# A graph layer on Trainium2: 29 or 35 of the node windows summed by matmul, the rest by gathered rows

## The chip, the cores and the metric

The kernel runs on one core of one Trainium2 chip. The metric is the device time of one execution in microseconds (us). Three runs of the kernel before gave 547.09, 547.55 and 548.72 us, median 547.55 us. The profiled execution is the one of 548.72 us.

## What is computed

There are 6,250 nodes with 128 features each and 100,000 edges, sorted by destination. Each edge has a type, 0 or 1. Every edge sends a linear image of its source's row, with one of two weight matrices by its type. The messages are summed by destination, the node's own image is added, and a ReLU, a residual and a layer norm follow:

```python
m_data = Xs @ W_data.T + b_data          # Xs = X[src]
m_ctrl = Xs @ W_control.T + b_control
msg = jnp.where((edge_types == 0)[:, None], m_data, m_ctrl)
agg = jax.ops.segment_sum(msg, dst, num_segments=X.shape[0])
out = jax.nn.relu(agg + (X @ W_self.T + b_self))
x = layernorm(x + out)
```

All of it is float32 in the reference.

## The kernel before, in words

**Preparation.** The images of all 6,250 nodes under both weight matrices are made first (L424 to L478). Each value is kept as three bfloat16 parts, so a row has 384 numbers. The rows lie in 98 blocks of 128: 49 blocks of nodes by two types. They stay in the on-chip tensor `m3`, and a copy goes to the tensor `table` in HBM (L476).

**Two ways of summing.** The nodes are divided in two. The first `NW` windows of 160 nodes each are summed by matmuls alone; the nodes behind them are summed in blocks of 128 by gathered rows.

*A window* (function `ranks`, then `sums`). Its edges (2,688 loaded, 21 to a partition) are first given places. The sort of L588 to L826 is done for a *group* of up to four windows at once. It walks 21 steps: DVE makes a one-hot mask of the source block of each edge (L644), PE adds it up against a triangle of ones (L654, eight matmuls of up to 392 columns in each step but the last, which has four), and DVE takes each edge's rank among the edges of the same block (L658). Masks at L673 and L679 and the scatter at L688 turn ranks into a list of 32 places for each source block, which goes to HBM and comes back as a broadcast to all partitions (`rows`, L838, 784 KB a window). Edges beyond 32 places, at most 64 a window, are listed by L725 to L791 and their rows are fetched by GpSimd (L796). The sums of one window then run over 25 sets of four source blocks:

- DVE turns the broadcast into masks (L846, two instructions a window) and makes the masks of destinations (L853, five a window);
- first stage, L866: four matmuls of 384 columns, each on a quarter of PE's columns, pick the rows of the edges out of `m3`;
- ACT copies the result from PSUM to SBUF as bfloat16 (L407; the planner may give it to DVE instead, L408);
- second stage, L880 and L883: four matmuls of 384 columns and three of 128 add the rows up by destination in the PSUM tile `a`.

There are two tiles `a` and three tiles `g` for the first stage.

*A gathered block* (function `gathered`, L902). Its edges are loaded as tiles of 128; a full block has 18 tiles. For each tile GpSimd fetches 128 rows of `table` by index (L958), six in flight, and PE adds them up by destination with four matmuls of 384 columns (L965) into the single PSUM tile `ga`. DVE makes the masks for six tiles at a time (L952). Eight short DVE instructions (L919 to L935) prepare up to four full blocks at once.

*The end of a window or block* (function `close`): DVE adds the three parts (L528), adds the residual (L537), takes the statistics (L541, L543) and a chain of short instructions (L554 to L567) makes the scale; ACT or DVE apply it (L572 to L579), and SP stores the result. In a group of windows the short chain is shared by four or five pieces, and in a gathered block it stands alone. The last 32 nodes of each window are closed together, one extra piece for each group but the first.

**The order of the work** is set at build time. Every operation is given to `Plan` (L84 to L188) with an engine, an estimated duration and a due time, and `Plan.run` simulates the engines and issues the operations in the order it finds. Windows are due every `TW` = 13 us. The sort of a group is due 58 us ahead of its first window and takes 1.8 us a step there. The gathered tiles are spread evenly between the third window and the last but one:

```python
g0, g1 = T0 + 2 * TW, T0 + (NW - 2) * TW
step = max((g1 - g0) / max(sum(GT), 20), 1.3)
```

**The numbers that the change touches** (L35 to L47):

```python
GROUPS = [1, 2] + [4] * 6 + [2]
NW = sum(GROUPS)
NGB = -(-(N - NW * WN) // P)
GT = [-(-(min(P, N - NW * WN - P * i) * 17) // P) + 1 for i in range(NGB)]
```

So there are 9 groups, 29 windows with 4,640 nodes, and 13 gathered blocks with the other 1,610 nodes: twelve of 128 nodes and 18 tiles, and one of 74 nodes and 11 tiles, 227 tiles in all. At the very end the matched edges are counted; were an edge not placed, the slow function `sums_over_all` would run over everything (L220 to L222).

Of the kernel before, what the change touches and what calls it, by code (L numbers as in the profile page):

```python
# [31 lines left out]
WN = 160  # L32
KT = 21
WIN = KT * P
GROUPS = [1, 2] + [4] * 6 + [2]  # L35
NW = sum(GROUPS)
R = 32
W4 = WN - P
# [45 lines left out]
class Plan:  # L84
# [6 lines left out]
    def add(self, engine, dur, fn, due, r=(), w=(), lat=0.0):  # L91
        alts = engine if isinstance(engine, list) else [(engine, dur, fn)]
        op = Op(alts, due, lat)
        op.index = len(self.ops)
        self.ops.append(op)
        deps = set()
        for items, writes in ((r, False), (w, True)):
            for item in items:
                b, key = item if isinstance(item, tuple) else (item, None)
                for k, (ws, rs) in b.keys.items():  # L100
                    if key is None or k is None or k == key:
                        deps.update(ws)
                        if writes:
                            deps.update(rs)
                if writes and key is None:
                    b.keys = {}
                ws, rs = b.keys.setdefault(key, ([], []))
                if writes:
                    b.keys[key] = ([op], [])
                else:  # L110
                    rs.append(op)
                if not b.users or b.users[-1] is not op:
                    b.users.append(op)
        deps.discard(op)
        op.deps = list(deps)
        return op
# [115 lines left out]
def sums_over_windows(ctx, tc, x, xt, edges, w, bias, out, total):  # L232
# [10 lines left out]
    table = dram.tile([NT * P, D3], BF16, name="table")  # L243
    packed = dram.tile([len(GROUPS), 2, P, NT], BF16, name="packed")

# [3 lines left out]
    def C(shape, dtype, name):  # L249
        return Buf(plan, const, shape, dtype, name, 1)  # L250
# [22 lines left out]
    def vec(due, cols, fn, r, w, rate=1.04):  # L273
        return add("DVE", dve(cols, rate), fn, due, r, w)
# [54 lines left out]
    for i in range(3):  # L329
        vec(0.3, P, lambda i=i: V.memset(one3.t[R * i : R * i + 1, :], 1.0), [], [one3], 0.3)  # L330
    counts = C([P, len(GROUPS) + NGB], F32, "counts")
    vec(2, 1, lambda: V.memset(counts.t, 0.0), [], [counts])
# [569 lines left out]
    def gathered(bis, when, step):  # L902

        nt, k_ = GT[bis[0]], len(bis)
        n = nt * k_
        gi = len(GROUPS) + bis[0]
        top = GB * max(GT)
# [67 lines left out]
    todo = []  # L975
    for gi, nw in enumerate(GROUPS):
        if gi == 0:
# [26 lines left out]
    total_ps = low()  # L1004
    nt = len(GROUPS) + NGB
    add("PE", 0.1, lambda: T.matmul(total_ps.t[:1, :nt], ones.t, counts.t, start=True, stop=True),
# [145 lines left out]
```

## Time and profile before

| | before |
|---|---|
| median of three runs | 547.55 us |
| profiled execution, its own time | 548.72 us |
| its span in the trace | 546.8 us |
| mean granted TensorE clock | 0.962 |
| PE / PEld busy | 483.3 / 380.5 us |
| DVE busy | 463.3 us, 1,615 instructions |
| ACT busy | 387.0 us |
| POOL busy | 252.2 us |
| 227 gathers of `t_msg` on POOL | 1,036 ns each |

PE is the matmul engine, PEld its weight loads, DVE the vector engine, ACT the scalar engine, POOL GpSimd, SP the engine that issues the transfers. Busy time is the union of an engine's instructions, so two that overlap are counted once. A group of instructions is shown as line, engine, operation, output and inputs with their shapes and count, then busy time and the mean duration of one in ns, then the idle time of the engine just before them and what ended it. A view by stages gives the busy time of each engine in stretches of the span, with the count of its instructions behind an x. The page's own chain of work that ended last is empty for this run.

### The profile page before, as it was taken

To read this page: it belongs to the slowest core of one execution; us is meant where nothing else is said; L and a number is where in the kernel's file an instruction comes from. 1 tells how busy PE (TensorE), PEld (TensorE's weight loads), DVE (VectorE), ACT (ScalarE), POOL (GpSimd) and SP (SyncE) were. 2 spreads that over 40 slices of the span, in tenths; PEclk is the share of its full clock that TensorE was granted. 3 is DMA by queue.
4 is the path that set the end of the run, shared out by engine and by line. 5 is a ranking of instruction groups with operands and counts; after the bars stand their busy time and mean duration, and the time that the engine had idled before them with its cause. 6 is when DMAs were issued, how large, how long until landed. Compare 5 with 4: busy or idle time off the path is not lost.

```text
span 546.8 us, 28398 instructions
## 1 busy us (share of the span) xinstructions
PE 483.3 (88%) x11972; PEld 380.5 (70%) x11972; DVE 463.3 (85%) x1615; ACT 387.0 (71%) x981; POOL 252.2 (46%) x251
## 2 busy tenths in 40 slices
PE   4996597998899899997999989998999999999891
PEld 2664364675578778786777777886778778887771
DVE  6885688899999999999999999899989987778603
ACT  2684464675577867777786877777777878888891
POOL 2000026413115766666556666566657667576000
PEclk9998888798799999999999999999999989999997
DMA  2689756404532474526652265426544265436100
GB/s 84 176 236 286 215 175 193 144 4 115 184 115 65 112 241 111 155 69 201 176 167 78 70 210 177 145 74 194 167 119 126 73 203 164 133 82 203 38 7 18
DMA packets 62714, 75.25 MB, mean 138 GB/s; under 512 B 19726, under 2 KB 52659, under 8 KB 62579
## 3 DMA queue, kind: packets, MB, share of 16 engines
q1 hardware_dynamic: 50497, 49.00, 28.7%
q0 software_dynamic: 11648, 23.87, 16.6%
q8 instruction: 95, 1.56, 1.2%
q10 hardware_dynamic: 434, 0.49, 0.3%
q14 instruction: 40, 0.33, 0.2%
HBM read 58.71 MB, written 13.20 MB: 132 GB/s over the span
## 4 chain that ended last, share of the span: by engine, by line


## 5 line engine op out<-in xcount | busy, mean ns | idle before, releaser
L407 ACT CAST gs<-g 128x384 bf16<-128x384 f32 x684 | 293.2, 480 | 89.5 <-PE g L866 81.3
L958 POOL DMA_INDIRECT t_msg<-table,t_idx x227 | 235.1, 1036 | 163.5 <-PE ga L965 93.6
L866 PE MATMUL g<-m,rows 128*32 128x384 bf16 x2842 | 272.3, 332 | 1.7 <-DVE rows L846 1.4
L880 PE MATMUL a<-gs,hot 128*32 128x384 bf16 x2784 | 264.2, 331 | 9.4 <-ACT gs L407 5.5
L866 PEld LDWEIGHTS <-rows 128*32 128x32 bf16 x2842 | 177.2, 135 | 17.3 <-DVE rows L846 2.8
L883 PE MATMUL a<-gs,hot 128*32 128x128 bf16 x2088 | 167.2, 220 | 1.1 <-issue 1.1
L880 PEld LDWEIGHTS <-hot 128*32 128x32 bf16 x2900 | 124.0, 96 | 36.5 <-issue 17.0
L658 DVE TENSOR_REDUCE slot<-rk 128x4 f32<-128x392 f32 (+2 forms) x189 | 90.4, 478 | 24.3 <-PE rk L654 19.8
L965 PE MATMUL ga<-t_msg,t_hot 128*32 128x384 bf16 x897 | 91.5, 331 | 2.3 <-DVE s L528 2.3
L883 PEld LDWEIGHTS <-hot 128*32 128x32 bf16 x2175 | 83.9, 97 | 7.1 <-issue 2.7
L654 PE MATMUL rk<-hots,tri 128*32 128x392 bf16 (+2 forms) x756 | 73.8, 309 | 7.6 <-DVE hots L644 7.6
L853 DVE TENSOR_TENSOR hot<-iota_b,to_d 128x800 bf16<-128x800 bf16 x145 | 76.6, 565 | 0.0
L654 PE MATMUL rk<-hots,rest 128*32 128x392 bf16 (+2 forms) x720 | 66.1, 311 | 9.6 <-DVE slot L658 8.4
L796 POOL DMA_INDIRECT sr<-table,at x15 | 14.4, 957 | 81.8 <-DVE t_far L931 65.8
L654 PEld LDWEIGHTS <-rest 128*32 128x32 bf16 x720 | 30.2, 96 | 31.1 <-issue 26.8
L644 DVE TENSOR_TENSOR hots<-iota_b,st 128x392 bf16<-128x392 bf16 (+2 forms) x189 | 51.3, 314 | 0.4 <-PE vt L688 0.2
L965 PEld LDWEIGHTS <-t_hot 128*32 128x32 bf16 x897 | 41.9, 98 | 6.7 <-issue 3.6
L654 PEld LDWEIGHTS <-tri 128*32 128x32 bf16 x756 | 32.4, 98 | 11.0 <-DVE tri L313 6.9
L846 DVE TENSOR_SCALAR rows<-rows,pid 128x1568 bf16<-128x1568 bf16 x58 | 37.8, 672 | 0.4 <-DMA rows<-packed 0.4
L528 DVE TENSOR_REDUCE s<-a 128x128 f32<-128x384 f32 x29 | 16.0, 553 | 24.8 <-ACT bs L407 15.2
L688 PEld LDWEIGHTS <-two 128*64 128x64 bf16 x609 | 16.0, 110 | 11.7 <-DVE two L679 5.8
L444 PE MATMUL g<-w_sb,xc 128*128 128x256 f32 x60 | 21.8, 454 | 2.2 <-DMA xc<-in_xt 2.2
(179 smaller groups left out, 567.7 us busy)
## 6 DMA issues: line engine op xcount, KB each, us to landing
rows<-packed SPq DMA_DIRECT2D x29, 784.0 KB
table<-m SPq DMA_DIRECT2D x12, 768.0 KB
t_msg<-table,t_idx POOLq DMA_INDIRECT x227
xc<-in_xt SPq DMA_DIRECT2D x11, 256.0 KB
xc<-in_xt SPq DMA_DIRECT2D x6, 320.0 KB
xr<-in_x SPq DMA_DIRECT2D x6, 256.0 KB
out<-xr SPq DMA_DIRECT2D x6, 256.0 KB
gl<-sr SPq DMA_DIRECT2D x29, 48.0 KB
```

The costliest lines, as they stand in the source:

```text
L407: [("ACT", act(cols), lambda: A.copy(o(), src())), ("DVE", dve(cols), lambda: V.tensor_copy(o(), src()))], None, None, due, r, w, lat)
L444: T.matmul(o, xa.t[:, at : at + P], w_sb.t[:, : 2 * D], start=i == 0, stop=False, skip_group_check=True)
L644: vec(due - (2.0 if k else 0.5), nw * NT, lambda k=k, hot=hot, k0=k0: V.tensor_tensor(hot.t[:, k - k0].rearrange("p w (c d) -> p w c d", d=2),
L654: T.matmul(acc.t[R * j : R * j + R, : nw * NT], wt.t[:, R * j : R * j + R], m, start=start, stop=stop, skip_group_check=True)
L658: vec(due, nw * NT, lambda k=k: V.tensor_reduce(slot.t[:, k, :], acc.t[:, : nw * NT].rearrange("p (w c) -> p w c", c=NT), axis=AX.X, op=AL ...
L846: add("DVE", dve(half * NT, 0.26), lambda sp=sp, rs=rs: V.tensor_scalar(sp.t[:, rs], sp.t[:, rs], pid1.t, None, op0=ALU.is_equal), due - 4 ...
L853: V.tensor_tensor(hot2.t[:, c0 : c0 + 5].rearrange("p g (c d) -> p g c d", d=2), iota1_b.t.rearrange("p (c d) -> p c d", d=2)[:, None].to_ ...
L866: T.matmul(gp.t[R * t : R * t + R, :D3], sp.t[:, :, 4 * g + t], m3.t[:, 4 * g + t, :], start=True, stop=True)
L880: T.matmul(a.t[R * j : R * j + R, :D3], hot2.t[:, g, R * j : R * j + R], gs.t, start=g == 0, stop=False, skip_group_check=True)
L883: T.matmul(a.t[R * c : R * c + R, D3:], hot2.t[:, g, P:], gs.t[:, c * D : (c + 1) * D], start=False, stop=last, skip_group_check=True)
L958: add("POOL", 1.25, lambda m=m, kk=kk: G.indirect_dma_start(out=m.t, out_offset=None, in_=table[:, :], in_offset=bass.IndirectOffsetOnAxis ...
L965: T.matmul(ga.t[R * i : R * i + R, :D3], hot.t[:, k % KB, R * i : R * i + R], m.t, start=k == 0, stop=False, skip_group_check=True)
```

## The change

One line is changed. The group of two windows at the end becomes a group of four, and one more group of four is added.

```diff
-GROUPS = [1, 2] + [4] * 6 + [2]
+GROUPS = [1, 2] + [4] * 8
```

All else follows from it: 10 groups and 35 windows with 5,600 nodes; 6 gathered blocks with the other 650 nodes (five of 128 nodes and 18 tiles, one of 10 nodes and 3 tiles), 93 tiles in all. The gathered tiles are planned 4.3 us apart instead of 1.43 us: (33 - 2) x 13 us over 93 tiles, before (27 - 2) x 13 us over 227. The full blocks are prepared four at a time and then one, before in three batches of four. No other line of the kernel differs.

## Prediction

> **What bounds the kernel now.** I read the busy shares of the page first, then the span cut into stages, then the DVE groups and the waits of the long middle stage. The page:
>
> ```profile
> PE 483.3 (88%) x11972; PEld 380.5 (70%) x11972; DVE 463.3 (85%) x1615; ACT 387.0 (71%) x981; POOL 252.2 (46%) x251
> PEclk9998888798799999999999999999999989999997
> ```
>
> No engine is idle enough to be ignored except POOL. The stages say more. I cut where the first window's sum starts (70), where the fourth window's sum leaves PSUM (157), after 17 more windows (424), where the last sort and gather are over (510), and at the last window's end (534.8):
>
> ```profile
> core 0: us, PE busy (x) PEld busy (x) DVE busy (x) ACT busy (x) POOL busy (x), PEclk, DMA share, GB/s
> 70.00:157.00 87.00, 75.73 (x1807) 55.52 (x1809) 80.33 (x277) 54.16 (x144) 28.43 (x28) 0.87 0.42 127
> 157.00:424.00 267.00, 250.12 (x6814) 206.62 (x6806) 252.37 (x813) 201.03 (x516) 165.78 (x160) 1.00 0.48 140
> 424.00:510.00 86.00, 82.66 (x2310) 68.93 (x2309) 67.02 (x234) 71.94 (x189) 55.23 (x55) 0.98 0.47 138
> 510.00:534.80 24.80, 21.60 (x586) 16.85 (x577) 9.84 (x37) 21.23 (x56) 0.00 (x0) 1.00 0.07 18
> 534.80:546.80 12.00, 0.89 (x10) 0.54 (x10) 4.34 (x24) 1.25 (x5) 0.00 (x0) 0.69 0.08 20
> ```
>
> In the 267 us of the middle DVE is busy 252.4/267 = 94.5% and PE 93.7%, ACT 75%, POOL 62%. Only there are windows, sorts and gathers all under way. The DVE groups of that stage show what fills it:
>
> ```profile
> L658 DVE TENSOR_REDUCE slot<-rk 128x4 f32<-128x392 f32 x91 | 50.5, 555 | 1.3 <-PE rk L654 1.3
> L853 DVE TENSOR_TENSOR hot<-iota_b,to_d 128x800 bf16<-128x800 bf16 x85 | 44.7, 566 | 0.0
> L644 DVE TENSOR_TENSOR hots<-iota_b,st 128x392 bf16<-128x392 bf16 (+1 forms) x96 | 28.7, 341 | 0.1
> L846 DVE TENSOR_SCALAR rows<-rows,pid 128x1568 bf16<-128x1568 bf16 x34 | 22.8, 687 | 0.4 <-DMA rows<-packed 0.4
> L952 DVE TENSOR_TENSOR t_hot<-iota_b,t_code 128x768 bf16<-128x768 bf16 x25 | 13.8, 551 | 0.0
> L528 DVE TENSOR_REDUCE s<-a 128x128 f32<-128x384 f32 x17 | 9.4, 552 | 4.0 <-ACT bs L407 1.0 <-PE ga L965 0.9 <-PE rk L654 0.9
> L528 DVE TENSOR_REDUCE s<-ga 128x128 f32<-128x384 f32 x9 | 4.7, 525 | 0.0
> ```
>
> The L528 rows count the work: 17 windows and 9 gathered blocks closed, so a window takes 267/17 = 15.7 us there. Almost nothing of DVE's groups has idle time ahead of it. The waits of the same stage:
>
> ```profile
> POOL t_msg L958 <- PE ga L965: 64.1, 57, 21.8
> ACT gs L407 <- PE g L866: 42.6, 79, 1.4
> POOL t_msg L958 <- PE g L866: 32.6, 47, 2.4
> ```
>
> POOL waits for PE, not PE for gathered rows: gathering isn't the bound, and taking it away removes no wait from the path. **DVE sets the pace, with PE close behind.**
>
> **The prices on DVE.** An instruction starts before its predecessor has ended, so means over-count. Two L853 in a row took 1.05 us in the trace; the second added 0.49. I charge the long ones their mean less 0.08 us (L853 0.49, L658 0.475, L644 0.26, L846 0.61, L528 0.48, L952 0.47; the masks of L673 and L679, 0.50, at 0.44), L537 0.26, L541 0.27, L543 0.17, and the dependent short ones (L554 to L567, 0.13 to 0.17) whole.
> - A gathered block of 18 tiles: three L952 1.41, one close 0.45 + 0.26 + 0.27 + 0.17 = 1.15, the short chain 7 x 0.15 = 1.05, in all 3.6 us; a preparation of 8 short instructions, about 1.6 us, stands for up to four blocks.
> - A window's sum and close: 5 x 0.49 + 2 x 0.61 + 0.48 + 0.26 + 0.27 + 0.17 + 0.1 = 4.95 us.
> - The sort of a group of four: 21 x (0.475 + 0.26) = 15.4; four times three masks 5.3; some 35 others about 7.5; the group's shared close and its extra piece 1.9. In all 30 us.
> - A group of four in place of two: the 196-column forms of L658 and L644 stand at 354 and 252 ns on the page by form, the 392-column ones at 556 and 354, so 21 x 0.30 = 6.4, and 3 for the other masks and lists.
>
> **The sum over the kernel on DVE.** Added: 6 x 4.95 + 30 + 9.4 = 69 us, and about 2 for casts of L408 that the planner now puts on DVE (17 casts of L408 in the built program for 12). Removed: 22 instructions L952 (38 to 16), 10.3; seven closes and short chains, 7 x 2.2 = 15.4; one preparation, 1.6; in all 27. Net +44, so 463 to 507 us. ACT gets 150 more casts at 0.48, +72 gross, but it has the room. POOL loses 134 gathers and gains 2, -137: worth nothing by itself.
>
> **The sum on PE.** In the tail one set of a window (two times four matmuls of 384 columns, three of 128) passes every 0.38 us:
>
> ```profile
> 531.00 0.35 PE L880 MATMUL a<-gs,hot 128*32 128x384 bf16 x4
> 531.16 0.24 PE L883 MATMUL a<-gs,hot 128*32 128x128 bf16 x3
> 531.18 0.38 PE L866 MATMUL g<-m,rows 128*32 128x384 bf16 x4
> 531.38 0.35 PE L880 MATMUL a<-gs,hot 128*32 128x384 bf16 x4
> ```
>
> Four matmuls of 384 columns are 384/896 of that, 0.165 us, which is what a gathered tile costs. So six windows add 6 x 25 x 0.385 = 58 us and the removed tiles give back 134 x 0.165 = 22: a window needs 25 x 0.385/160 = 60 ns of PE per node, a full gathered block 18 x 0.165/128 = 23 ns. The change moves 960 nodes from the cheaper form to the dearer one on PE, DVE and ACT alike. Only POOL is relieved.
>
> **The end, by stages.** In the order of the built program PE has the same 18 gathered tiles and the same 71 sort steps up to the end of the fourth window, so **0 to 157 us stays**. The last sort is again over four or five windows before the end: 26 windows (the fifth to the thirtieth) with sorts beside them, then five without.
> - The 26 windows. Before, DVE had 252.4/17 = 14.85 us a window with 9 tiles. Without gathered work that is (252.4 - 25 x 0.47 - 9 x 2.2 - 4)/17 = 12.75; sorts are slightly thinner (5.13 steps a window by the built order, 5.26 before), -0.2; the 74 tiles left in this stretch, some 17 us over 26 windows, +0.65. So 13.2 us a window, 343 in all. PE, by the pace above, had 9.6 for the sets, 1.5 for 9 tiles, 5.26 x 2 x 392/896 x 0.385 = 1.8 for sort steps and, as I estimate from the counts, 1.4 for scatter, lists and own rows, 14.3 a window; it goes to 9.6 + 0.5 + 1.7 + 1.2 = 13.0. DVE was 94.5% busy with PE at 14.3/14.85 of it; now the two are closer, and I take 93.5%: 14.1 us a window, **367 us**.
> - Five windows without sorts. Before: 24.8 us for two, and 13 us for the one from 497 to 510, less 8 tiles at 0.165. About 12 us each, **60 us**. PE alone would need 25 x 0.385 + 0.7 = 10.3, the lower end.
> - The last close: **12 us**, the same chain.
>
> Sum 157 + 367 + 60 + 12 = 596 us of span; 1.9 us lie outside it (548.72 - 546.8), 598 against the profiled run's 548.7, which is 1.2 above the median. **Forecast: 597 us.** Cross-check: 507 us of DVE, less 49.4 before 70 (the same view) and some 30 after the sorts (9.8 for two windows now, 4.3 for the close), are 428 us in 157 - 70 + 367 = 454, 94%.
>
> Unseen before: groups that follow more densely on SP (6 more broadcasts of 784 KB, 4.7 MB, and 13 MB less gathered; DMA was 48% busy in the middle, so no cost), and gathered tiles that are few and come in bursts. What a window then waits for I bound by both ends: no slack lost (DVE 97% busy, 354 us) and no slack won (15.7 us a window as now, 408 us). I stay near the lower end, since almost no wait on PE or DVE names a gather.
>
> **A rule of the skill weighed.** L846 took 687 ns in the middle and 627 between 70 and 157, where POOL worked less; L853 566 and 564. By these rows, fewer gathers are worth 58 x 0.06 = 3.5 us at most. The Trainium skill, "SBUF — State Buffer", section "Who interferes with whom", says that some DVE instructions and GpSimd lock each other out of a shared port pair for a whole instruction; if each of the 134 gathers had held DVE up for its 1.04 us, 139 us would come back and the kernel would be faster. The rows show no such hold.
>
> **Rivals.**
> 1. *The gathers were free filler* (0.13): they filled holes that windows leave anyway, and a window stays at 15.7. 157 + 408 + 60 + 12 + 2 = 639; half of it, 618, is where it begins. For: PE and DVE both have 6% holes. Against: DVE's groups show no idle time that gathers could fill.
> 2. *PE and DVE pack better with fewer queues* (0.15): 13.3 us a window and 10.5 in the five last, 346 + 53 + 171 = 570.
> 3. *The other side* (0.02), one mechanism: DVE's instructions shrink in the middle for want of GpSimd's traffic. Not slower needs (547.5 - 157 - 60 - 12 - 2)/26 = 12.2 us a window, so DVE's 13.2 us shorter by 8% and no hole left. L853's 566 ns with gathers and 560 without (510 to 534) speak against it.
> 4. *It doesn't do what it says* (under 0.01): an added window might hold too many edges and the slow function run, milliseconds. The inputs settle it: of the added windows the fullest has 2,676 edges of 2,688, and at most 43 edges of 64 overflow the lists.
>
> **Chances.** The forecast 0.70, the others as given. The range takes in half of the filler case and the better packing: 570 to 617. A measurement of this kernel tells 0.3% from no change: faster 0.02, within 0.01, slower 0.97.
>
> **What would show it.** Right: some 14 us a window in the middle with DVE over 92% busy, DVE about 507 us in all, POOL about 116. Wrong: L853 or L658 shorter by several per cent (rival 3); a window at 15 us or more with DVE under 90% (rival 1); an early stage that no longer ends at 157.

## The result, and the profile after

The kernel after takes 614.43 us (median of four runs, 613.06 to 616.28), beside 548.13 us for the kernel before: a ratio of 1.1206, 95% interval 1.116 to 1.1252. The forecast was 597 us, in a range of 570 to 617. The profiled execution took 616.28 us, with a span of 614.6 us. The page of the kernel after, the rows that answer to those shown of before:

```profile
PE 536.3 (87%) x13418; PEld 422.3 (69%) x13418; DVE 506.8 (82%) x1681; ACT 446.9 (73%) x1134; POOL 118.2 (19%) x120
PEclk9999785999999999999999999999999999999996
```

All engines but POOL did more. DVE came to 506.8 us where the sum of instructions said 507, POOL to 118 where it said about 116. ACT gained 60 us where the sum said 72, and PE 53 where sets and tiles alone gave 58 - 22 = 36, a sum that left out the added sort steps. So the instructions of the engine that the forecast rests on were priced well, and the difference lies in how they fit together. The stages of the kernel after, cut at the same events (first sum, end of the fourth window, 424, end of the last window with a sort beside it, end of the last window); the columns are the stretch, its length, busy time and count of each engine, granted clock, DMA share and GB/s:

```profile
core 0: us, PE busy (x) PEld busy (x) DVE busy (x) ACT busy (x) POOL busy (x), PEclk, DMA share, GB/s
67.00:157.80 90.80, 78.76 (x1836) 56.96 (x1837) 79.75 (x278) 54.40 (x144) 27.73 (x28) 0.86 0.44 129
157.80:424.00 266.20, 247.64 (x6768) 204.02 (x6770) 248.62 (x785) 210.70 (x544) 63.45 (x61) 1.00 0.35 102
424.00:538.20 114.20, 105.42 (x2912) 88.54 (x2908) 97.19 (x293) 90.12 (x233) 23.34 (x22) 1.00 0.31 94
538.20:598.40 60.20, 54.95 (x1448) 41.99 (x1438) 27.69 (x83) 53.20 (x137) 0.95 (x1) 1.00 0.20 64
598.40:614.60 16.20, 0.88 (x16) 0.54 (x16) 4.03 (x18) 1.47 (x5) 0.00 (x0) 0.67 0.10 26
```

The start is as before (157.8 against 157.0). The 26 windows with sorts take 266.2 + 114.2 = 380.4 us, 14.63 each; DVE is busy 345.8 us of them, 90.9%. The five windows without sorts take 60.2 us, and the last close 16.2 us instead of 12.0. What DVE did in the 380 us, and whom it waited for:

```profile
L658 DVE TENSOR_REDUCE slot<-rk 128x4 f32<-128x392 f32 x137 | 76.4, 558 | 12.7 <-PE rk L654 9.8 <-PE ga L965 1.5 <-PE g L866 0.9
L853 DVE TENSOR_TENSOR hot<-iota_b,to_d 128x800 bf16<-128x800 bf16 x130 | 68.4, 562 | 0.0
L846 DVE TENSOR_SCALAR rows<-rows,pid 128x1568 bf16<-128x1568 bf16 x50 | 30.6, 642 | 3.8 <-DMA rows<-packed 3.8
L528 DVE TENSOR_REDUCE s<-a 128x128 f32<-128x384 f32 x25 | 13.8, 554 | 5.0 <-ACT bs L407 3.9 <-PE rk L654 0.6 <-PE a L883 0.3
```

The mean durations are those of before, to 1%, except L846 (642 ns for 687). The idle time ahead of L658 has grown. It is 12.7 us here, and in the answering stretch of before (157 to 497.2 us, 22 windows) 1.3 + 5.8 us, most of it in the last sort, a group of two windows:

```profile
L658 DVE TENSOR_REDUCE slot<-rk 128x4 f32<-128x392 f32 x95 | 52.7, 555 | 1.3 <-PE rk L654 1.3
L658 DVE TENSOR_REDUCE slot<-rk 128x2 f32<-128x196 f32 x21 | 7.4, 353 | 5.8 <-PE rk L654 5.5 <-issue 0.3
```

So in the sorts of four windows, where DVE hardly waited for PE before, it now does.

### The profile page after: what moved, and what is told of

It is laid out like the page before. It is cut to its first block, busy times and chain, and to the rows that moved or that the text cites. A ratio compares the mean times of both kernels' runs of the same rounds, so it can differ in the third digit from the quotient of the medians.

```text
span 614.6 us, 31394 instructions
## 1 busy us (share of the span) xinstructions
PE 536.3 (87%) x13418; PEld 422.3 (69%) x13418; DVE 506.8 (82%) x1681; ACT 446.9 (73%) x1134; POOL 118.2 (19%) x120
## 4 chain that ended last, share of the span: by engine, by line
PE 43%; DVE 38%; DMA 8%; ACT 4%; issue 4%; POOL 0%; SPq 0%; ACTq 0%; DVEq 0%; POOLq 0%
PE a L880 13%; PE g L866 12%; DVE slot L658 6%; DVE hot L853 6%; PE rk L654 6%; DVE hots L644 4%; DMA xc<-in_xt 4%; ACT gs L407 3%; DVE two L679 2%; PE g L444 2%; PE a L883 2%; DVE rows L846 2%; DMA rows<-packed 2%; PE vt L688 2%; DVE s L528 2%
## 5 line engine op out<-in xcount | busy, mean ns | idle before, releaser
L407 ACT CAST gs<-g 128x384 bf16<-128x384 f32 x824 | 350.1, 480 | 90.1 <-PE g L866 80.2
L880 PE MATMUL a<-gs,hot 128*32 128x384 bf16 x3360 | 315.0, 330 | 15.1 <-ACT gs L407 6.3
L866 PE MATMUL g<-m,rows 128*32 128x384 bf16 x3430 | 326.1, 329 | 1.5 <-ACT gl L407 0.6
L866 PEld LDWEIGHTS <-rows 128*32 128x32 bf16 x3430 | 224.0, 134 | 14.8 <-issue 1.9
L883 PE MATMUL a<-gs,hot 128*32 128x128 bf16 x2520 | 206.1, 219 | 1.1 <-issue 1.1
L880 PEld LDWEIGHTS <-hot 128*32 128x32 bf16 x3500 | 149.9, 95 | 56.8 <-issue 28.4
L958 POOL DMA_INDIRECT t_msg<-table,t_idx x93 | 97.9, 1053 | 159.1 <-PE ga L965 144.3
L658 DVE TENSOR_REDUCE slot<-rk 128x4 f32<-128x392 f32 (+2 forms) x210 | 106.6, 508 | 26.5 <-PE rk L654 21.3
L883 PEld LDWEIGHTS <-hot 128*32 128x32 bf16 x2625 | 105.1, 96 | 6.5 <-issue 2.6
L853 DVE TENSOR_TENSOR hot<-iota_b,to_d 128x800 bf16<-128x800 bf16 x175 | 92.5, 563 | 0.1
L528 DVE TENSOR_REDUCE s<-a 128x128 f32<-128x384 f32 x35 | 19.4, 554 | 37.4 <-PE a L883 21.6
L846 DVE TENSOR_SCALAR rows<-rows,pid 128x1568 bf16<-128x1568 bf16 x70 | 42.5, 637 | 8.6 <-DMA rows<-packed 8.6
L654 PEld LDWEIGHTS <-tri 128*32 128x32 bf16 x840 | 37.9, 98 | 12.3 <-DVE tri L313 6.8
L965 PE MATMUL ga<-t_msg,t_hot 128*32 128x384 bf16 x363 | 38.2, 343 | 3.4 <-DMA t_msg<-table,t_idx 1.5
L688 PEld LDWEIGHTS <-two 128*64 128x64 bf16 x735 | 19.0, 110 | 14.2 <-DVE two L679 10.2
L688 PE MATMUL vt<-hots,two 128*64 128x98 bf16 x735 | 24.6, 211 | 3.5 <-DVE two L679 3.4
```

Source lines behind the costliest of these rows:

```text
L407: [("ACT", act(cols), lambda: A.copy(o(), src())), ("DVE", dve(cols), lambda: V.tensor_copy(o(), src()))], None, None, due, r, w, lat)
L654: T.matmul(acc.t[R * j : R * j + R, : nw * NT], wt.t[:, R * j : R * j + R], m, start=start, stop=stop, skip_group_check=True)
L658: vec(due, nw * NT, lambda k=k: V.tensor_reduce(slot.t[:, k, :], acc.t[:, : nw * NT].rearrange("p (w c) -> p w c", c=NT), axis=AX.X, op=AL ...
L688: T.matmul(vv()[q : q + 64, i // 2, :], two.t[:, (k - k0) * nw + i].rearrange("p f r -> p (f r)"), hot.t[:, k - k0, i, :], start=k == 0 an ...
L846: add("DVE", dve(half * NT, 0.26), lambda sp=sp, rs=rs: V.tensor_scalar(sp.t[:, rs], sp.t[:, rs], pid1.t, None, op0=ALU.is_equal), due - 4 ...
L853: V.tensor_tensor(hot2.t[:, c0 : c0 + 5].rearrange("p g (c d) -> p g c d", d=2), iota1_b.t.rearrange("p (c d) -> p c d", d=2)[:, None].to_ ...
```

## The experiments

**Which chip a run fell on matters here.** The kernel before was timed again beside the experiments. On one chip it took 549.77 us, close to the 548.13 of the result; on two others it took 672 to 680 us, and one of these repeated it (672.3 and 672.06 us). Call the former the fast chip and the latter the slow ones. What differs between them is open. Where no gathered tiles run, the two kinds agree as far as can be seen. The window from the seventh L528 to the eighth, which has no tiles in the kernel after, takes 14.81 us there and 14.81 us in the windows alone, run on a slow chip. The last four windows of the spread kernel below, behind all but its last gather, take 48.6 us on a slow chip and 48.7 on the fast one. No whole kernel without gathered tiles was timed on both.

### Windows alone

The gathered blocks are left out, and so are the 650 (or 1,610) nodes that they make. The edit is shown for 35 windows; for 29 it is made in the kernel before, with 74181 in place of 89518.

```diff
-    for b0 in range(0, NGB, GB):
+    for b0 in range(0, 0, GB):
...
-    with tc.If(matched != E), ExitStack() as rest:
+    with tc.If(matched != 89518), ExitStack() as rest:
```

> The kernel after without its six gathered blocks (93 tiles): the last 650 nodes are left out of the output, and the final count is compared with the 89,518 edges of the windows. Theory of bursts (DVE sets the pace; the 18 tiles of a block are bunched in three of six windows, so windows that PE bounds alternate with windows that DVE bounds): DVE is left with about 12.6 us a window in the middle, 13.4 at 94%, so 26 windows give back 32 us, the first four 4 us: about 578 us. Theory of filler (the gathers fill holes that windows leave; a window costs about 14.4 whether or not tiles run beside it, as the windows without tiles in the trace of after do): about 606 us.

> The kernel before without its 13 gathered blocks (227 tiles): the last 1,610 nodes are left out of the output, and the final count is compared with the 74,181 edges of the windows. Theory of bursts (DVE pace): 22 windows with sorts at 13.5 us, 153 ahead of them, 36 for the last three, 14 at the end: about 500 us, so that the 227 tiles cost 0.2 us each. Theory of filler: windows stay at 14.4, about 520 us, 0.12 us a tile. Both: the gap to the 35 windows is 6 windows, 80 to 88 us.

Measured, on a slow chip: 597.72 us with 35 windows (596.02 to 599.12) and 510.96 us with 29 (509.52 to 512.04). **A window costs (597.72 - 510.96)/6 = 14.5 us**, and beside these, the gathers cost 614.43 - 597.72 = 16.7 us for 93 tiles (0.18 each) and 548.13 - 510.96 = 37.2 us for 227 (0.16 each). The prices of the gathers take these kernels to need the same time on the chip of the result, which is shown for parts only. The measured 66.3 us are by this 6 x 14.5 = 86.8 us for the windows less 37.2 - 16.7 = 20.5 us for the gathers. That divides the difference in two; it is no check of it, since the same four times stand on both sides. The times lie between the theory of filler (606 and 520) and that of bursts (578 and 500), a little nearer to the former. The stage with sorts, 26 windows of the 35 and 22 of the 29:

```profile
151.80:523.70 371.90, 343.71 (x9368) 282.65 (x9361) 331.84 (x1021) 298.71 (x768) 13.56 (x14) 1.00 0.27 84
152.70:461.40 308.70, 286.32 (x7864) 234.37 (x7860) 269.76 (x858) 251.65 (x649) 10.98 (x11) 1.00 0.26 82
```

In the first DVE has 331.84/26 = 12.8 us of work a window, near the 12.6 expected; but a window takes 14.3, so that DVE is busy 89.2%. Against the kernel after, DVE has 345.8 - 331.8 = 14.0 us less to do in the 26 windows, and these are 380.4 - 371.9 = 8.5 us shorter: two fifths of what was freed became idle time.

### The gathered tiles spread evenly

The six blocks come in bursts in the built order of the kernel after: PE meets 18 tiles in about three windows, then none for three. The edit ties each gather to the first stage of the window at its due time, which makes it three tiles in every window (so the traces show it):

```diff
-    T0 = 36.0
+    T0 = 36.0; marks = {}
...
-                add("PE", 0.165, stage1, d, [sp] + m3_key(g), [gp])
+                marks[w0 + i, g] = add("PE", 0.165, stage1, d, [sp] + m3_key(g), [gp])
...
-                    at, [idx, table_b], [m], lat=2.0)
+                    at, [idx, table_b], [m], lat=2.0).after.append(marks[divmod(int((at - T0) / TW * NS), NS)])
```

> The kernel after with the gathered tiles held back at build time so that PE meets three in every window, where it met 0 to 10. Same instructions. Theory of bursts: PE and DVE are evenly loaded, 14.1 us a window instead of 14.6, about 601 us, DVE 93 to 94% busy in the middle. Theory of filler: no change beyond 3 us, 611 to 616 us.

> The kernel after, unaltered, beside the kernel before on whatever chip this call gets, since the calls' own times of the kernel before differ (548 us, then 672 us beside the first four experiments). If the kernel before takes about 548 us again, the ratio is 1.12 and the time 614 us. If it takes about 672 us: where that comes from PE waiting for nothing that the profile shows while gathers run beside the windows, the kernel after with 93 gathered tiles instead of 227 should lose less than the 124 us, some 50 us, and come out at 650 to 680 us, close to the kernel before.

> The even spread of the gathered tiles once more, now beside the kernel after on one chip. Theory of bursts: 10 to 14 us faster than the kernel after. Theory of filler: within 3 us of it. A third theory, from the first run of this kernel (23 us for every fourth window, in which PE got its instructions in small pieces while transfers filled the DMA engines): slower than the kernel after on a chip where the kernel before takes 672 us.

The first run came out at 697.93 us, on a slow chip, beside 672.3 us for the kernel before, so it tells nothing on its own. The second had the kernel after beside it on the fast chip: 618.1 us spread, 614.47 us not (ratios to the kernel before 1.1243, interval 1.119 to 1.1296, and 1.1187, interval 1.1132 to 1.1241). Its 26 windows with sorts:

```profile
160.20:542.00 381.80, 357.76 (x9698) 291.03 (x9700) 344.05 (x1079) 301.91 (x775) 103.31 (x87) 1.00 0.33 101
```

They take 14.68 us each with DVE 90.1% busy, where the theory of bursts wanted 14.1 and 93 to 94%. **The theory of bursts has fallen**: an even spread gains nothing; it loses 3.6 us, which is also slightly more than the 3 that the theory of filler allowed. The kernel after repeated its time within 0.1 us.

### More work for DVE, more work for PE

Both are made in the kernel of windows only, without a change of order. The first makes three of the five destination masks of each window twice, the second does the first stage of 8 of the 25 sets twice:

```diff
+                    for _ in range(2 if c0 in (0, 10, 20) else 1)],
```

```diff
+                    for _ in range(2 if g % 3 == 1 and not last else 1):
```

> The kernel of windows only (35 windows, 597.7 us; the last 650 nodes are left out) with three of the five masks of L853 made twice in each window: 105 more DVE instructions of 0.49 us, 51 us of DVE work in the same order. If DVE sets the pace, the 26 middle windows take 1.47 us longer each and the whole is 38 to 51 us slower, 636 to 649 us. If PE sets it and DVE has 11% to spare there, less than 15 us. If they wait for each other in turn, between.

> The kernel of windows only with the first stage (L866) of 8 of the 25 sets of each window done twice: 32 more matmuls of 384 columns a window, 8 x 0.165 = 1.32 us of PE a window, 46 us in all, in the same order. If PE sets the pace, 34 to 46 us slower, 632 to 644 us. If DVE sets it, less than 15 us over the middle and the 1.32 us only in the five windows without sorts, 605 to 615 us. If they wait for each other in turn, between.

Measured, on the fast chip: 643.87 us with more DVE work (+46.2 over the windows alone) and 616.55 us with more PE work (+18.8). The stages with sorts, DVE's first, then PE's:

```profile
157.30:568.00 410.70, 349.10 (x9363) 280.56 (x9358) 374.88 (x1099) 298.60 (x769) 13.28 (x13) 1.00 0.25 76
```

```profile
152.40:535.60 383.20, 370.35 (x10186) 320.74 (x10181) 332.26 (x1020) 307.36 (x767) 13.01 (x13) 1.00 0.26 81
```

With 374.88 - 331.84 = 43.0 us more of DVE work the stage is 38.8 us longer: nine tenths of it show. With 26 x 1.32 = 34.3 us more of PE work by price (26.6 by PE's busy time) it is 11.3 us longer: a third or two fifths show. The middle so fits the case in which DVE sets the pace (under 15 us), while the whole came out 1.5 us above the 605 to 615 given for it. **In the windows alone DVE sets the pace, as the forecast said**, and PE holds it up at times. DVE was 91.3% busy in the first of the two; with more work than in the kernel after it still had 9% of holes.

### Two sorts under way

```diff
-        F = lambda name, dt=F32: B(work, [P, KT, nw], dt, name, 1, rm)
-        F2 = lambda name: B(work, [P, KT, nw, 2], BF16, name, 1, 2 * rm)
+        F = lambda name, dt=F32: B(work, [P, KT, nw], dt, name, 2, rm)
+        F2 = lambda name: B(work, [P, KT, nw, 2], BF16, name, 2, 2 * rm)
...
-        hots = [B(work, [P, ks[c + 1] - ks[c], nw, NT], BF16, f"hots{c}", 1,
+        hots = [B(work, [P, ks[c + 1] - ks[c], nw, NT], BF16, f"hots{c}", 2 if c < 2 else 1,
...
-        acc = B(ps, [P, 512], F32, "rk", 1)
+        acc = B(ps, [P, 512], F32, "rk", 2)
```

> The kernel of windows only (35 windows, 597.7 us; the last 650 nodes are left out) with a second buffer for the sort's tiles and a second PSUM bank for its ranks, which the missing gathers leave free, so that the sort of one group may overlap the next. Same instructions. Theory of coupling (DVE sets the pace, but without gathered work to fill in it stands at 89% because the 21 steps of the one sort under way make DVE and PE wait for each other in turn): DVE rises to 92 to 94% in the middle, a window takes 13.6 to 13.9 us instead of 14.3, 578 to 588 us. If the holes come from elsewhere: 595 to 600 us.

Measured, on a slow chip like the kernel with one sort: 578.59 us (576.44 to 581.17), 19.1 us less. The time is the one that the theory of coupling gave, but it is not where that theory put it. The stages up to the fourth window's end and behind it, one sort and then two:

```profile
0.00:151.80 151.80, 126.67 (x2191) 84.73 (x2195) 123.96 (x474) 91.61 (x218) 6.53 (x13) 0.89 0.48 147
151.80:523.70 371.90, 343.71 (x9368) 282.65 (x9361) 331.84 (x1021) 298.71 (x768) 13.56 (x14) 1.00 0.27 84
```

```profile
0.00:134.70 134.70, 116.27 (x2190) 80.66 (x2194) 119.58 (x464) 90.20 (x218) 6.61 (x13) 1.00 0.55 166
134.70:502.10 367.40, 344.15 (x9366) 280.10 (x9359) 333.13 (x1027) 298.87 (x772) 12.64 (x14) 1.00 0.27 85
```

The first four windows end 17.1 us sooner, and the granted clock stays at 1.00 there instead of 0.89. The 26 windows win 4.5 us, 14.13 us each instead of 14.30, with DVE at 90.7%; the theory wanted 13.6 to 13.9 us and 92 to 94%. DVE's holes there shrank from 40.1 us to 34.3. So in the middle the single sort accounts for a small part of them only. What the other part comes from is not settled. That the time fell into the stated range was luck.

### Fewer windows, and the other chips

```diff
-GROUPS = [1, 2] + [4] * 8
+GROUPS = [1, 2] + [4] * 6
```

and, for 31 windows, `[4] * 7`.

> The change turned round: groups 1, 2 and six of 4, 27 windows and 16 gathered blocks (282 tiles). By the prices on DVE: two windows less, 10 us, a sort of two less, 20 us, 55 tiles more, 12 us: DVE 445 us instead of 463, and 547.5 x 445/463 gives 526 us, unless POOL's last tiles, of which 24 stand behind the last window, become the end: then up to 550 us. Theory of filler, which holds gathers to be nearly free: two windows at 15.5 less, 516 us, with the same reserve on POOL.

> 27 windows and 282 gathered tiles once more, on this call's chip. By the prices that the runs without gathers gave (14.5 us a window, 0.165 us a tile): 548 - 2 x 14.5 + 55 x 0.165 = 528 us, if POOL keeps up; by the forecast's prices on DVE 526 us. If POOL's last tiles, of which 24 stand behind the last window, become the end: 545 to 560 us.

> 31 windows and 183 gathered tiles (groups 1, 2 and seven of 4), between the kernel before and the kernel after. By the prices of the runs without gathers: 548 + 2 x 14.5 - 44 x 0.165 + 4 for the longer last close = 574 us. By the prices that the forecast implied (13.2 us a window, 0.21 us a tile): 548 + 26 - 9 = 565 us.

> 27 windows and 282 gathered tiles, a third time: both runs so far fell on a chip where the kernel before takes 672 us. If this call's chip runs the kernel before in about 548 us: 528 us by the prices of the runs without gathers, if POOL keeps up, and 545 to 560 us if its last 24 tiles become the end; the former would beat both kernels. If the chip is the other again: 710 us.

All four fell on slow chips, where the kernel before takes 672 to 680 us. 27 windows took 708.71, 710.04 and 719.21 us there, ratios of 1.0533 (interval 1.0484 to 1.0582), 1.0544 (1.049 to 1.0598) and 1.0593 (1.0533 to 1.0653). 31 windows took 676.22 us, ratio 1.0047 (1.0008 to 1.0086). On these chips gathers are dear: 227 tiles make 672.3 - 510.96 = 161 us, 0.71 us each, and neither price above holds. The 93 tiles of the spread kernel make 697.93 - 597.72 = 100 us, 1.08 each, so no single price holds there. With 27 windows the last tiles also became the end, as the expectation had in reserve: in the first of these runs the last window's L528 starts at 664.8 us of a span of 706.7, and 42 us with gathered tiles still to sum follow. There, fewer windows are slower. Whether 27 windows beat the kernel before where that takes 548 us was not seen, and neither was the kernel after on the other chips.

The spread kernel ran on both kinds, with the same instructions, so its traces show where the time goes. The seventh window, on the slow chip (23.5 us) and on the fast one (13.9 us):

```profile
198.30:221.80 23.50, 17.00 (x355) 12.34 (x345) 12.67 (x38) 11.57 (x28) 9.39 (x10) 0.78 0.47 143
```

```profile
189.50:203.40 13.90, 12.74 (x356) 10.76 (x345) 12.45 (x38) 11.29 (x29) 11.46 (x9) 1.00 0.69 217
```

As many instructions, nearly the same busy time of DVE and ACT, but 0.78 of the clock and long stretches in which PE does nothing. Of the waits of PE over the whole run "issue", the engine waiting for nothing that the profile shows, grew most; the slow chip first:

```profile
PEld L880 <- issue: 82.9, 163, 4.2
```

```profile
PEld L880 <- issue: 33.3, 100, 2.0
```

The POOL instructions of the gathers were no slower (1,081 ns on the slow chip, 1,198 on the fast one). The first 5.7 us of that window, slow chip first:

```profile
198.30:204.00 5.70, 2.92 (x43) 1.48 (x34) 2.20 (x9) 1.03 (x3) 4.48 (x5) 0.85 0.99 341
```

```profile
189.50:195.20 5.70, 5.70 (x172) 4.97 (x164) 5.57 (x16) 5.52 (x15) 4.48 (x5) 1.00 0.93 330
```

On the slow chip transfers fill the DMA engines (0.99, 341 GB/s) while PE goes on in small pieces; but on the fast one they are nearly as full (0.93, 330 GB/s) and PE works without a break. So full DMA engines alone don't explain it. That PE's instructions come late there would fit, but no run tested it, and why PE stands still is open.

## Why the prediction was right, and what its size missed

The direction and the bound were right, and the range held, by 2.6 us: the forecast said 49.5 us more, the change cost 66.3, and 614.43 lies close to the 618 at which rival 1 was to begin. The forecast's own sign of being right, 14 us a window with DVE over 92% busy, was not met (14.63 us, 90.9%), nor was that of rival 1 (15 us or more, under 90%). Against the measured span of 614.6 us the forecast's span of 596 us misses 18.6 us, step by step:

- **"0 to 157 us stays"**: 157.8, +0.8.
- **Work of DVE, 343 us in the 26 windows and 507 in all**: 345.8 and 506.8. Right.
- **"I take 93.5%"**, the share of time that DVE would be busy: 90.9%, so 380.4 us instead of 367, **+13.4. This is the step that failed.** The 94.5% it started from came from 157 to 424 us, the best part of the stretch with sorts. In the trace of before it can be read for the whole stretch, to the end of the last window with a sort beside it, and for the last five windows of it alone:

```profile
157.00:497.20 340.20, 320.43 (x8796) 265.45 (x8792) 310.86 (x1022) 261.52 (x674) 214.79 (x208) 0.99 0.48 139
424.00:497.20 73.20, 70.31 (x1986) 58.82 (x1986) 58.49 (x209) 60.49 (x159) 49.00 (x49) 0.98 0.47 136
```

  The whole is 310.86/340.2 = 91.4%, 15.46 us a window, and 343/0.914 gives 375 us, 5 from the truth. The last windows with sorts run thinner in DVE in both kernels (58.5/73.2 = 80% before, 97.2/114.2 = 85% after). Before, their work on DVE falls from 14.85 to 11.7 us a window and the window only from 15.7 to 14.6. PE is 96% busy there, which points to PE and not DVE as the one that sets the pace; no run tested it.

  Counted by the window, DVE's mean idle time didn't change: (340.2 - 310.9)/22 = 1.33 us before and (380.4 - 345.8)/26 = 1.33 us after. Added to the forecast's 13.2 us of work, it gives 14.5 us a window and 378 us, closer than either share. Two equal means are no rule: in the first 17 of the windows of before it was (267 - 252.4)/17 = 0.86 us.
- **"A gathered tile costs 0.165 us on PE"**, and 0.2 by the prices on DVE: 0.16 to 0.18 in time. PE's figure was close to the time, which does not show that PE set it. On DVE a tile took (506.8 - 483.2)/93 = 0.25 us of work (483.2 is the 35 windows alone), of which 0.18 shows.
- **"Five windows without sorts, 60 us"**: 60.2. Right.
- **"The last close: 12 us, the same chain"**: 16.2, +4.2. The chain is not the same: the last group now has four windows, and their extra piece of 128 rows is stored in four parts, not two, so SP is done 1.1 us later after the last window's end (12.3 against 11.2 us). And POOL's closing DRAIN lasted 9.2 us instead of 2.5 and ended 3.1 us behind SP. In the 35 windows alone, which have the longer group but a DRAIN of 1.6 us, the last L528 starts 14.2 us ahead of the span's end, in the kernel after 16.1 and before 11.9; so by that reading about half of the 4.2 us comes with the group.

*Rival 1, gathers as free filler*, put a window at 15.7 us. It was wrong as stated: the windows became shorter, 14.63. Its mechanism was there in part, as the windows alone show: DVE's holes were 1.33 us a window in both kernels with gathers, 40.1/26 = 1.54 us in the 35 windows alone and 38.9/22 = 1.77 in the 29 (as shares 8.6, 9.1, 10.8 and 12.6%). So gathered work filled some of them, and taking a part of it away did not yet widen them. *Rival 2* (13.3 us a window) and *rival 3* (DVE's instructions shrink) were wrong: L853 took 566 ns before, 562 after and 563 without any gather.

The rule weighed in the forecast, of the Trainium skill, "SBUF — State Buffer", section "Who interferes with whom", names the forms that can contend with GpSimd, `tensor_scalar` among them. L846 is one, and its mean went from 687 ns to 642 with fewer gathers and 617 with none. By the rows that is about 2 us in this kernel. The direction fits the rule and the size is small; no run tells the shared port from other causes.

## What to carry to other kernels

Price the work of an engine by its instructions, but take the time that it stands idle from the whole stretch that the change makes longer, the thin end of it included, not from its best part, and try it by the window as well as by the share. Work taken away beside a bound comes back as time only in part: here 0.18 us for 0.25 us of DVE work. And a change of how work is divided between two ways should be timed on more than one chip, since the price of one way was some 0.17 us a tile on one and 0.71 on another.

## What the runs showed of the hardware

- POOL's last DRAIN took 9,215 ns in all four traces with 93 gathered tiles (the kernel after twice, the spread twice), on both kinds of chip alike, 2,518 ns in the kernel before, and 1,374 and 1,620 ns without gathered tiles. It ended the span in the first four. It doesn't follow the number of tiles: with 183 it took 7,663 ns and with 282 in all three traces 6,193. What sets it is open.
- The same program took 618.1 us on one chip and 697.9 on another, with PE standing at "issue" for long and the mean clock granted to it 0.917 instead of 0.965. It was seen only in kernels with gathered tiles beside the windows.
- The granted clock changed with the order of the work: where two sorts overlapped, the first 134.7 us had 1.00, with one sort the first 151.8 us had 0.89, with the same instructions. The share of time that PE is busy doesn't tell it by itself: it was 86% and 83% there, and from 70 to 157 us of the kernel before 87% at a clock of 0.87.
